# Five edits to an eight-stage network: first fill on ScalarE, causal mask on VectorE, six tiles of the ternary feed-forward begun early, expert weights by broadcast transfers

## The chip, the cores and the metric

The kernel runs on one core of one Trainium2 chip. The metric is the device time of one launch in microseconds (us), as the median of several runs. PE is the matmul engine (TensorE), DVE is VectorE, ACT is ScalarE, POOL is GpSimd, and SP is SyncE, which here mostly issues transfers. Each engine takes its own instructions in order and waits on semaphores for what other engines or transfers must have done.

## The reference, cut to what matters

The input `x` has 32 sequences of 64 rows and 256 columns, 2048 rows in all; `ctx` has the same shape. Four layers follow, each with an attention part and a feed-forward part, and each part adds its result to `x`:

```python
LN = _layernorm
x = x + L0_xattn(LN(x), ctx, ctx, gamma)  # A: 8 heads of 8 over the 64 rows, softmax over 256 columns
x = x + L0_ffn(LN(x))                     # B: gated feed-forward, 704 wide
x = x + L1_xattn(LN(x), ctx)              # C: 16 heads of 16, fake-quantised, softmax over all 2048 rows
x = x + L1_ffn(LN(x))                     # D: a block: causal attention, then 4 experts, top 2
x = x + L2_xattn(LN(x), ctx)              # E: 8 heads of 8 over 256 columns, |i - j| <= 64
x = x + L2_ffn(LN(x))                     # F: ternary feed-forward
x = x + L3_xattn(LN(x), ctx, ctx)         # G: sigmoid attention
x = x + L3_ffn(LN(x))                     # H: 8 experts, top 2, and shared experts
```

The parts that the change touches are these, shortened:

```python
# D, attention of each sequence, 16 heads of 128, after rotary encoding
scores = einsum('bhqd,bhkd->bhqk', q, k) / sqrt(128)
probs  = softmax(where(causal, scores, most_negative))
out    = einsum('bhqk,bhkd->bhqd', probs, v)

# F
rmsnorm(x, g)  = g * x * rsqrt(mean(x * x) + 1e-8)
act_quant(x)   = round(x * 127 / max|x|) / (127 / max|x|)     # one scale for each row
linear(x, w, g) = act_quant(rmsnorm(x, g)) @ ternary(w).T
out = linear(silu(linear(x, w1, g1)) * linear(x, w2, g2), w3, g3)   # 256 -> 1024 -> 256

# H
topk_w, topk_i = top_k(softmax(x @ gate_w.T), 2)
combine = zeros(N, 8), with topk_w at topk_i
h  = silu(x @ w_gate[e]) * (x @ w_up[e])                      # 8 experts, 176 wide
y  = sum over e of combine[:, e] * (h @ w_down[e])
y += (silu(x @ sw_gate) * (x @ sw_up)) @ sw_down              # shared, 352 wide
```

## The kernel before, in words

**Tiles and order.** The 2048 rows are 16 tiles of 128 rows by 256 columns, kept in SBUF through all stages as `xs[0]` to `xs[15]`; NG = 4 groups of four tiles are used where a matmul takes 512 rows. The stages run one after the other in the order A to H; G is done inside F's loop. On an engine the instructions stand in the order of the program. In A, C, E, F and the experts of D this order is written out by hand, under `tc.manual_schedule()`.

**A and E: `attention_slots`.** Both use one loop of slots `t`. Tile `i` begins its preparation at t = 8i - 2 and its score maxima at t = 8i + 16, its attention units at t = 8i + 30, its products at t = 8i + 32, and its normalisation and residual (`finish`) from t = 8i + 40 on; the loop ends at t = 180. A hook `start(t)` lets a stage put other work in a slot. The q and k of a tile are split into three bfloat16 parts, written to DRAM (`stacked`, d3q and d3k) and read back as stacked rows (`stack_rows`) into one of four buffer pairs `stk` and `stq`. These have their upper 64 rows filled once, with ones and with zeros (`operand_buffers`). In A (`row` is None) the fill is a DVE memset, L158, of the pair that belongs to each of the tiles 0 to 3, when the tile is prepared. In E the fill is a transfer from a filled row. All transfers of `stacked` and `stack_rows` (L212 and L220) are on SP's queue. The scores' maxima are matmuls (L251) with a DVE reduction each (L255); the exponentials are on ACT (L287).

**D attention.** 64 units, each one head by one group of 512 rows (four tiles). In slot `u` the PE does the product of unit u-4, the transposes of u-3, the scores of u-2 (`scores`), an output product, and the projections of unit u with their rotary encoding, which take DVE (`rtq`, `rtk`), ACT (`rwq`, `rwk`) and POOL. In `scores` the mask is a matmul: `identb` times `causalb`, L1097, is accumulated into the same PSUM bank as the four products q k (L1100). DVE then reduces the maximum (L1102), subtracts it (L1104), ACT takes one exponential over 128x512 (L1105), DVE sums (L1107), inverts (L1108) and multiplies (L1109).

**F.** `run_F` loops over slots t = 0 to 23. The list `parts` gives the order of steps in a slot, each with its lag in tiles. The first six steps of a tile, here called its front, are `deviations` (mean and variance, L1468), `first_factors` (factors with POOL's power), `first_sizes` (two products with gains, L1499, maximum and scales), `first_rounding` (two ACT activations), `first_transposes` (four on PE) and `first_copy` (ACT, L1521, giving `xT`). Then come `hidden_products` (L1529, eight matmuls) and `hidden` (L1544). The weights and gains of F are reserved and loaded in the stages ahead, in a pool `wp`.

**H.** For each group, 14 chunks of 128 columns of the experts' widths: chunks 0 to 10 are the routed experts (8 x 176 = 1408 columns), 11 to 13 the shared ones. A chunk is four matmuls for gate and up (L1844), for a routed chunk one matmul `cb` (L1848), and eight for the down product of the chunk before (L1820, `hout`). The routing weights of a group stand in `share`, in three bfloat16 parts; `cb` multiplies them with `owner`, a matrix of zeros and ones that says which column belongs to which expert, and so spreads them over the chunk's 128 partitions. DVE makes `hm` from up and silu(gate) (L1854), then multiplies it by `cb` (L1856). `owner` is filled by three ACT copies in F's last slots (L1760).

Of the kernel before, what the change touches and what calls it, by code (L numbers as in the profile page):

```python
# [9 lines left out]
F32 = mybir.dt.float32  # L10
# [7 lines left out]
P = 128  # L18
T = 2048
D = 256  # L20
# [11 lines left out]
def tile_net(ctx: ExitStack, tc: tile.TileContext, a: dict, out: bass.AP):  # L32
# [119 lines left out]
    def operand_buffers(pool, k, b, row=None):  # L152

        pair = {}
        for kind, value in (("k", 1.0), ("q", 0.0)):
            pair[kind] = pool.tile([P, 16, D], BF, name=f"st{kind}{b}")
            if row is None:
                V.memset(pair[kind][64:P], value)  # L158
            else:

                nc.sync.dma_start(pair[kind][64:P], bc(row[kind][64:P], 1, [64, 16, D]))
# [32 lines left out]

    def stacked(pool, k, dram, src, kind, i):
# [15 lines left out]
        for t in range(n):  # L211
            nc.sync.dma_start(d3[t].rearrange("d h c -> h d c"), t3[:, t % 3, :])  # L212
        return d3

    def stack_rows(k, d3, kind, i):
        st = k["st"][i % 4][kind]
        for m in range(3):
            first = 0 if kind == "q" else m
            src = d3[first : first + 3].rearrange("t d h c -> (t d) (h c)")
            nc.sync.dma_start(st[24 * m : 24 * m + 24], src)  # L220
# [807 lines left out]
    def run_D_attention(w, side, hs):  # L1028
# [4 lines left out]
        with ExitStack() as es:  # L1033
# [5 lines left out]
            causal = tpool.tile([P, 4, P], BF, name="causalb")  # L1039
            V.tensor_copy(causal, bc(w["causal"], 1, [P, 4, P]))  # L1040
# [53 lines left out]
            def scores(u):  # L1094
                qr, kr = qks.pop(u)
                sp = psum.tile([P, 4, P], F32, tag="sp", name="sp")
                PE.matmul(sp, identb, causal, start=True, stop=False, skip_group_check=True)  # L1097
                for j in range(4):
                    js = slice(j * P, (j + 1) * P)
                    PE.matmul(sp[:, j, :], qr[:, js], kr[:, js], start=False, stop=True, skip_group_check=True)  # L1100
                mx = pool.tile([P, 4], F32, name="mx")
                V.tensor_reduce(mx, sp, AX.X, ALU.max)  # L1102
                s = pool.tile([P, 4, P], F32, name="s", bufs=3)
                V.tensor_tensor(s, sp, bc(mx, 2, [P, 4, P]), ALU.subtract)  # L1104
                S.activation(s, s, AF.Exp, scale=scale)  # L1105
                sm = pool.tile([P, 4], F32, name="sm")
                V.tensor_reduce(sm, s, AX.X, ALU.add)  # L1107
# [178 lines left out]
    def first_of_E(w, psum):  # L1286
# [5 lines left out]
        for kind, value in (("k", 1.0), ("q", 0.0)):  # L1292
            row[kind] = cp.tile([P, D], BF, name=f"row{kind}")
# [35 lines left out]
    def run_E(w, side):  # L1329
        bd = w["bd"]  # L1330
        with ExitStack() as es:
# [38 lines left out]
            attention_slots(pool, psum, k, band, SCALE8, prepare, values, finish, early=EARLY)  # L1370
# [55 lines left out]
    def load_F(wp):  # L1426
# [3 lines left out]
        w["g3"] = bcast_row(wp, a["L2_ffn_g3"], 1024, "fg3")  # L1430
        return w

    def run_F(w, side):
# [10 lines left out]
        at = shared["atanh"]  # L1444
        t1, t2, t3 = (t.rearrange("p (c n) -> p c n", c=c) for t, c in zip(shared["tern"], (2, 2, 8)))
        with tc.tile_pool(name="Ft", bufs=1, side=side) as tpool, tc.tile_pool(
            name="Fw", bufs=2, side=side
        ) as pool, tc.tile_pool(name="Fp", bufs=1, space=PSUM) as psum, tc.manual_schedule():
            up = tpool.tile([P, 1], F32, name="rndup")
            V.memset(up, RND)  # L1450
            down = tpool.tile([P, 1], F32, name="rnddown")
            V.memset(down, -RND)
            st = [{} for _ in range(NT)]
            head = iter(())

            U = 1e-4 / 127.0
            base = [[tpool.tile([P, n + 1], F32, name=f"base{nm}{b}") for b in range(2)] for nm, n in (("a", 2), ("b", 1))]
            for tiles, lo in zip(base, (0, 2)):  # L1460
                for t in tiles:
# [506 lines left out]
```

## Time and profile before

| what | value |
|---|---|
| median of three runs | 2762.11 us (2757.15 to 2770.57) |
| the profiled execution | 2769.85 us, of which the instructions span 2768.1 us |
| mean granted TensorE clock | 0.977 of full speed |
| busy: PE | 2414.7 us (87%), its weight loads 1431.1 us |
| busy: DVE, ACT, POOL | 1856.7 us (67%), 1532.9 us (55%), 1534.5 us (55%) |
| A begins its first score product | 24.64 us |
| D attention | about 1205 to 1820 us, 9.31 us for one slot |
| E ends (last write of `x`) | 2276.0 us |
| H begins | 2453.5 us |

All times within the profile are counted from the start of its span. A row of the timeline reads: start, duration, engine, line and operation, what it writes and what it reads, the shape, how many were merged, and in brackets how long the engine sat idle before it and what ended the wait. A row of windows gives for one stretch the busy time of each engine with the number of instructions, then the granted clock, the share of DMA and GB/s. The lines are shown with the prediction, each where it is used.

### The profile page before, as it was taken

Reading aid. Unit: us, or ns where it says so; the run is one execution under the profiler, and the core shown is the slowest. Engines: PE = TensorE matmul, PEld = TensorE weight load, DVE = VectorE, ACT = ScalarE, POOL = GpSimd, SP = SyncE. Lnnn points to the kernel's source line nnn. Section 1 sums busy time; section 2 is a strip of 40 time slices with the busy share of each in tenths; the row PEclk is TensorE's granted clock in tenths of the full one; section 3 lists DMA queues with packets and bytes.
Section 4 is the critical chain, followed back from the end, with each engine's and each line's share of the span. In section 5 each row is a group of like instructions: output and inputs, shape, how many; then the busy total and the mean of one; then the engine's idle time right before and its main releaser. Section 6 shows DMA issues by size and latency. Waiting matters only on the chain.

```text
span 2768.1 us, 44270 instructions
## 1 busy us (share of the span) xinstructions
PE 2414.7 (87%) x15971; PEld 1431.1 (52%) x16078; DVE 1856.7 (67%) x3913; ACT 1532.9 (55%) x2181; POOL 1534.5 (55%) x1764
## 2 busy tenths in 40 slices
PE   4999889777777777779999999999888877789999
PEld 2555344344444444436666666666555544455565
DVE  7878555799999999955454554655577758833232
ACT  1666321699999999836555555534254557731111
POOL 4565533588888888865555555513488866710000
PEclk9999999999999999989999999999999998989999
DMA  6543000599999999930000000051343311000000
GB/s 166 133 116 86 24 1 1 120 204 204 202 204 200 203 206 201 204 106 1 16 8 23 8 1 1 1 107 52 79 99 90 93 46 55 1 0 8 8 8 8
DMA packets 618919, 227.89 MB, mean 82 GB/s; under 512 B 547494, under 2 KB 608844, under 8 KB 614092
## 3 DMA queue, kind: packets, MB, share of 16 engines
q1 hardware_dynamic: 615628, 224.26, 37.1%
q8 instruction: 127, 2.08, 0.3%
q10 hardware_dynamic: 3072, 0.79, 0.2%
q14 instruction: 92, 0.75, 0.1%
HBM read 66.91 MB, written 18.87 MB: 31 GB/s over the span
## 4 chain that ended last, share of the span: by engine, by line
PE 47%; DVE 19%; issue 9%; POOL 6%; ACT 2%; DMA 1%; ACTq 0%; POOLq 0%; DVEq 0%
DVE e L844 11%; PE yp L1141 4%; PE ppq L1082 4%; PE ppk L1082 4%; PE pgate L1844 4%; PE pup L1844 4%; PE hout L1820 3%; PE vp L1070 3%; POOL e L295 2%; PE sp L1100 2%; PE op L1126 2%; PE hmp L1198 2%; PE ep L1211 2%; PE sc L816 1%; PE op L805 1%
## 5 line engine op out<-in xcount | busy, mean ns | idle before, releaser
L868 ACT ACTIVATE ei<-e,nb,sq 128x2048 int16<-128x2048 f32 x256 | 535.4, 2092 | 39.6 <-DVE nb L865 35.0
L878 POOL CAST eb<-ei 128x2048 bf16<-128x2048 int16 x256 | 482.0, 1893 | 110.7 <-ACT ei L868 92.7
L816 PE MATMUL sc<-kT,qz 128*128 128x512 bf16 x930 | 281.0, 381 | 154.6 <-DVE e L844 150.6
L255 DVE TENSOR_REDUCE negm<-s 128x2 f32<-128x512 f32 (+1 forms) x512 | 300.7, 610 | 129.1 <-PE s L251 126.3
L844 DVE TENSOR_SCALAR_CACHE_REDUCE e<-sc,mx 128x1024 f32<-128x1024 f32 x256 | 326.1, 1274 | 0.4 <-DVE nb L865 0.3
L287 ACT ACTIVATE e<-s 128x1024 f32<-128x1024 f32 (+1 forms) x256 | 233.4, 916 | 152.4 <-PE s L283 103.5
L844 DVE TENSOR_SCALAR_CACHE_REDUCE e<-sc 128x1024 f32<-128x1024 f32 x256 | 312.4, 1220 | 4.8 <-PE sc L816 4.8
L816 PEld LDWEIGHTS <-qz 128*128 128x128 bf16 x1024 | 94.6, 97 | 260.0 <-issue 202.3
L251 PE MATMUL s<-stk,stq 96*128 96x256 bf16 (+1 forms) x1024 | 192.2, 271 | 41.0 <-DMA d3k<-t3k 24.6
L1090 POOL TENSOR_TENSOR rwq<-rwq,sin 128x512 f32<-128x512 f32 x64 | 81.1, 1267 | 239.2 <-ACT rwq L1087 212.3
L283 PE MATMUL s<-stq,stk 128*128 128x256 bf16 (+1 forms) x1024 | 180.8, 262 | 11.0 <-DMA d3k<-t3k 8.4
L829 PEld LDWEIGHTS <-vz 128*64 128x64 bf16 x4096 | 122.7, 109 | 113.7 <-issue 112.7
L1854 DVE TENSOR_TENSOR hm<-pup,sl 128x512 f32<-128x512 f32 (+1 forms) x56 | 38.7, 691 | 200.2 <-PE pup L1844 197.5
L1087 ACT ACTIVATE rwq<-ppq,dbq 64x512 f32<-64x512 f32 x128 | 87.4, 683 | 153.6 <-DVE rtq L1084 150.0
L1102 DVE TENSOR_REDUCE mx<-sp 128x4 f32<-128x512 f32 x64 | 44.3, 692 | 190.8 <-PE sp L1100 190.8
L829 PE MATMUL av<-eT,vz 128*64 128x128 bf16 x4096 | 163.2, 222 | 9.3 <-DMA eT<-eb 6.8
L251 PEld LDWEIGHTS <-stq 96*128 96x128 bf16 x1024 | 94.0, 101 | 131.6 <-issue 108.7
L305 PE MATMUL o<-e,vmo 128*32 128x256 f32 (+1 forms) x2048 | 150.7, 366 | 6.2 <-POOL e L295 4.8
L295 POOL TENSOR_SCALAR_AFFINE_SELECT e<-e 128x256 f32<-128x256 f32 (+1 forms) x256 | 132.9, 546 | 30.5 <-ACT e L287 30.3
L1852 ACT ACTIVATE sl<-pgate 128x512 f32<-128x512 f32 (+1 forms) x56 | 33.4, 597 | 207.9 <-PE pgate L1844 207.8
L91 POOL TENSOR_TENSOR rstd<-ve,mhalf 128x1 f32<-128x1 f32 (+1 forms) x40 | 25.9, 646 | 185.3 <-DVE ve L89 83.7
L1070 PE MATMUL vp<-Dwv,hnT 128*128 128x512 f32 x256 | 122.2, 600 | 6.1 <-ACT hnT L949 5.5
(406 smaller groups left out, 5443.1 us busy)
## 6 DMA issues: line engine op xcount, KB each, us to landing
stk<-d3k SPq DMA_DIRECT2D x96, 192.0 KB
stq<-d3q SPq DMA_DIRECT2D x96, 192.0 KB
d3k<-t3k SPq DMA_DIRECT2D x160, 64.0 KB
d3q<-t3q SPq DMA_DIRECT2D x96, 64.0 KB
eT<-eb SPq DMA_TRANSPOSE x256
fw<-in_L_ffn_w SPq DMA_DIRECT2D x3, 1024.0 KB
x<-in_x SPq DMA_DIRECT2D x16, 128.0 KB
c<-in_ctx SPq DMA_DIRECT2D x16, 128.0 KB
```

The lines of the kernel that those rows point to most:

```text
L251: PE.matmul(sc[:, hh, lo:hi], qs[0:96, 2 * hp + hh, qc * P : (qc + 1) * P], ks[0:96, 2 * hp + hh, lo:hi], start=band is None, stop=True, s ...
L255: V.tensor_reduce(negm[:, qc, 2 * hp : 2 * hp + 2], sc[:, :, lo:hi], AX.X, ALU.max, negate=True)
L287: S.activation(e[:, :, lo:hi], sc[:, :, lo:hi], AF.Exp, scale=scale)
L295: G.affine_select(e[:, :, s0:s1], e[:, :, s0:s1], [[0, 4], [step, s1 - s0]], ALU.is_ge, 0.0, base=base, channel_multiplier=chan,)
L816: PE.matmul(sc[:, k0 : k0 + 512], qz[i % 2][:, h, :], kT[:, h // 2, 1024 * part + k0 : 1024 * part + k0 + 512], start=True, stop=True,)
L829: PE.matmul(av[i][r0 : r0 + 64, h // 4, :], vz[:, kt, h // 4, h % 4, :], eT[:, kt, :], start=h == 0 and kt < 2, stop=h == H - 1 and kt >= ...
L844: V.tensor_scalar(e, scs.pop((n, part)), 1.0, mx[:, 0:1] if part else LOWEST, ALU.mult, ALU.max, accum_out=mx[:, part : part + 1],)
L868: S.activation(ei, es_.pop(n), AF.Exp, bias=nb, scale=sq[i][:, h : h + 1], accum_out=sums[i][:, h : h + 1],)
L878: G.tensor_copy(eb, eis.pop(n - 1))
L1070: PE.matmul(vp, hnT[g][:, c, j * P : (j + 1) * P], wv[:, c, :], start=c == 0, stop=c == 1)
L1082: PE.matmul(pp, wt[:, c, hh * P : (hh + 1) * P], hnT[g][:, c, :], start=c == 0, stop=c == 1)
L1844: PE.matmul(pp[:m], w[nm + "s"][:, c, cols], xnT[:, c, :], start=c == 0, stop=c == 1)
```

## The change

1. A's fill: `operand_buffers` fills the upper rows with `S.mul` of a row of ones by 1 or 0, on ACT, in place of the DVE memset.
2. A's transfers: for tile 0 the six transfers of q are issued from ACT's queue in place of SP's.
3. D's mask: the mask matmul and its bfloat16 tile go. DVE adds the mask while it brings the scores from PSUM to SBUF, reduces the maximum from there and scales it by -scale; ACT takes four exponentials of 128x128, each with its row's bias, and accumulates the sums on the way.
4. F's front: `front_of_F` holds the six steps, and `early_F` runs them for the tiles 0 to 5 from slot t = 147 of E on, two of the six steps of one tile in each slot, with `xT` and the scales `dqa` kept in `wp` and the transposes in PSUM under the tag "s1" of the score maxima. F's loop starts at t = 1 and leaves out the fronts of these tiles.
5. H's weights: `owner`, `share` in three parts and `cb` go. The routing weights of a group, 8 x 512 float32, are written to DRAM, and for every routed chunk SP issues one or two broadcast transfers into `wc` (128 x 512 float32, four buffers), three chunks ahead. The shared chunks stand first in each group.

```diff
@@ operand_buffers
             if row is None:
-                V.memset(pair[kind][64:P], value)
+                dst = pair[kind][64:P].rearrange("p h (a c) -> p (h a) c", c=P)
+                S.mul(dst, bc(ones[64:P], 1, [64, 32, P]), value)
...
+    def queue_of(k, kind, i):
+        return nc.scalar if kind == "q" and i == 0 and "row" not in k else nc.sync
...
-            nc.sync.dma_start(d3[t].rearrange("d h c -> h d c"), t3[:, t % 3, :])
+            queue_of(k, kind, i).dma_start(d3[t].rearrange("d h c -> h d c"), t3[:, t % 3, :])
...
-            nc.sync.dma_start(st[24 * m : 24 * m + 24], src)
+            queue_of(k, kind, i).dma_start(st[24 * m : 24 * m + 24], src)
@@ scores, D attention
-                PE.matmul(sp, identb, causal, start=True, stop=False, skip_group_check=True)
                 for j in range(4):
                     js = slice(j * P, (j + 1) * P)
-                    PE.matmul(sp[:, j, :], qr[:, js], kr[:, js], start=False, stop=True, skip_group_check=True)
+                    PE.matmul(sp[:, j, :], qr[:, js], kr[:, js], start=True, stop=True)
+                s = pool.tile([P, 4, P], F32, name="s", bufs=3)
+                V.tensor_tensor(s, sp, bc(w["causal"], 1, [P, 4, P]), ALU.add)
                 mx = pool.tile([P, 4], F32, name="mx")
-                V.tensor_reduce(mx, sp, AX.X, ALU.max)
-                s = pool.tile([P, 4, P], F32, name="s", bufs=3)
-                V.tensor_tensor(s, sp, bc(mx, 2, [P, 4, P]), ALU.subtract)
-                S.activation(s, s, AF.Exp, scale=scale)
+                V.tensor_reduce(mx, s, AX.X, ALU.max)
+                V.tensor_scalar(mx, mx, -scale, None, ALU.mult)
                 sm = pool.tile([P, 4], F32, name="sm")
-                V.tensor_reduce(sm, s, AX.X, ALU.add)
+                for j in range(4):
+                    S.activation(
+                        s[:, j, :], s[:, j, :], AF.Exp, bias=mx[:, j : j + 1], scale=scale, accum_out=sm[:, j : j + 1]
+                    )
@@ E's end
-            attention_slots(pool, psum, k, band, SCALE8, prepare, values, finish, early=EARLY)
+            front = []
+            def start(t):
+                if t == 147 and "F" in heads and "ternary" not in shared:
+                    front.append(heads.pop("F")(lambda name: psum.tile([P, 2, 2, P], F32, tag="s1", name=name, bufs=2)))
+                if front:
+                    next(front[0], None)
+            attention_slots(pool, psum, k, band, SCALE8, prepare, values, finish, start, early=EARLY)
...
+    FRONT = 6
+    def early_F(w, bank):
+        def own(shape, dt, name, i, bufs=2):
+            keep = name in ("xT", "dqa")
+            return w["wp"].tile(shape, dt, name=f"{name}_{i}" if keep else f"early_{name}", bufs=1 if keep else bufs)
+        fronts = front_of_F(w, own, bank)
+        w["done"] = FRONT
+        for s in range(FRONT + 2):
+            for k in range(3):
+                if 0 <= s - k < FRONT:
+                    for part in fronts[2 * k : 2 * k + 2]:
+                        part(s - k)
+                    yield
@@ run_F
-            for t in range(NT + 8):
+            for t in range(1 if done else 0, NT + 8):
                 for part, lag in parts:
+                    if part in fronts and t - lag < done:
+                        continue
...
-                    if with_g and t >= NT + 1 and part.__name__ == "gained":
-                        next(heads.get("owner", head), None)
@@ H
+        sh = pool.tile([8, 512], F32, name="sh")
+        S.copy(sh, tp[0:8].rearrange("e j t -> e (j t)"))
+        w["shares"][g] = w["dram"].tile([8, 512], F32, name="shd")
+        nc.sync.dma_start(w["shares"][g], sh)
...
+            ORDER = [11, 12, 13] + list(range(11))
+            def weights_of(n):
+                g, ch = divmod(n, 14)
+                ch = ORDER[ch]
+                if ch < 11:
+                    wc = wcs[n] = pool.tile([P, 512], F32, name="wc", bufs=4)
+                    e, r0 = ch * P // 176, 0
+                    while r0 < P:
+                        r1 = min(P, 176 * (e + 1) - ch * P)
+                        nc.sync.dma_start(wc[r0:r1], w["shares"][g][e : e + 1, :].to_broadcast([r1 - r0, 512]))
+                        e, r0 = e + 1, r1
...
-                    if ch < 11:
-                        cb = psum.tile([P, 512], F32, tag="cb", name="cb")
-                        PE.matmul(cb, owner[:, cols], sh, start=True, stop=True)
+                if n + 3 < 14 * NG:
+                    weights_of(n + 3)
...
-                    if ch < 11:
-                        V.tensor_tensor(hm, hm, cb, ALU.mult)
+                if n in wcs:
+                    V.tensor_tensor(hm, hm, wcs.pop(n), ALU.mult)
```

## The prediction

> **What bounds the kernel now.** I read the strip of forty slices first, then windows of the four touched stretches, then the timeline inside one slot of each.
>
> ```profile
> span 2768.1 us, 44270 instructions
> PE   4999889777777777779999999999888877789999
> DVE  7878555799999999955454554655577758833232
> ACT  1666321699999999836555555534254557731111
> 1280.00:1800.00 520.00, 518.61 (x2302) 346.78 (x2302) 275.42 (x466) 282.70 (x456) 283.04 (x226) 1.00 0.03 8
> 2249.50:2276.50 27.00, 18.46 (x178) 9.11 (x170) 9.82 (x20) 12.70 (x19) 16.60 (x31) 0.96 0.01 2
> 2276.50:2320.10 43.60, 27.30 (x103) 13.31 (x107) 34.15 (x104) 25.16 (x43) 21.37 (x32) 0.67 0.42 125
> 2453.50:2768.00 314.50, 310.78 (x1024) 182.89 (x1024) 88.33 (x180) 48.34 (x75) 8.81 (x11) 0.99 0.02 7
> ```
>
> A digit is the busy tenths of a 69 us slice. The window rows give stretch, length, busy us of PE, PE's weight loads, DVE, ACT, POOL, then clock and DMA. D's attention (1280 to 1800) and H (from 2453.5) are PE: 518.6 of 520 and 310.8 of 314.5, at full clock, with DVE and ACT about half used or less. There a PE instruction is worth its time. E's end has DVE at 9.8 of 27 us; F's start has DVE at 34.2 of 43.6, PE at 27.3 and a clock of 0.67: DVE is the limit, beside a pipeline that fills. Stage A's start is PE and ACT waiting:
>
> ```profile
> 24.64 1.01 PE L251 MATMUL s<-stk,stq 96*128 96x256 bf16 x4 [24.64 <-DMA d3k<-t3k]
> 26.87 3.47 DVE L158 MEMSET stk<- 64x4096 bf16 x1 [0.91 <-issue]
> 33.25 1.18 PE L251 MATMUL s<-stk,stq 96*128 96x256 bf16 x4 [6.66 <-DVE negm L255]
> 51.68 1.18 PE L251 MATMUL s<-stk,stq 96*128 96x256 bf16 x4 [6.61 <-DVE negm L255]
> 41.40 1.28 ACT L457 ACT_TABLE_LOAD   x1 [41.40 <-PE cT L101]
> 59.05 1.02 ACT L287 ACTIVATE e<-s 128x1024 f32<-128x1024 f32 x1 [14.17 <-DMA d3k<-t3k]
> ```
>
> Twice PE waits 6.6 us for a maximum (`negm`) queued on DVE behind two fills, and ACT does nothing until 41.4.
>
> **1, zeros on ACT, q's DMAs on ACT's queue (A): -6, from -11 to 0.** Eight DVE fills (3.47 and about 1.76) go; four of them, the two pairs at 26.87 and 45.29, lie behind PE's waits, so up to 2 x 5.6 = 11 comes free. ACT gains eight fills of 64x4096. The row for 128x2048 on ACT is 2.09 us, so twice that, 4.2 each, 33 us in all. The Trainium skill ("ScalarE: Activation LUTs", section "What ACT_TABLE_LOAD costs") gives an immediate-scale form 186 ns + 0.833 N ns, an estimate of 3.6 each or 29 us. Its section "Rules for kernel authors" speaks against the change: plain multiplies belong on VectorE. By that rule the move costs 29 for about 21 removed; by the trace those 29 to 33 fall into ACT's idle 41. I side with the trace, but not fully: the last fill ends near 33 to 40, and ACT's copies of cT and of the maxima, at 41.4 to 44 before, then come near 44. The row DMAs of tile 0's q wait on ACT behind two fills (8 us) and for t3q, and should issue at 18 to 20, against 16.61 on SP; the first product waited for k's transfers to 24.64, so it hardly moves (a late q costs 0 to 4). SP has six issues fewer ahead of tile 1's. The first exponentials at 59.05 move to about 50; tile 2's rows, still behind weight loads on SP (46.82), give 2 or 3 back. Hence -6.
>
> **2, causal mask on DVE (D): -13, from -14.5 to -8.**
>
> ```profile
> 1401.54 0.38 PE L1097 MATMUL sp<-causalb,identb 128*128 128x512 bf16 x1
> 1401.75 1.05 PE L1100 MATMUL sp<-rtk,rtq 128*128 128x128 f32 x8
> 1404.29 0.63 ACT L1105 ACTIVATE s<-s 128x512 f32<-128x512 f32 x1 [1.61 <-DVE s L1104]
> 1407.36 1.38 ACT L1087 ACTIVATE rwq<-ppq,dbq 64x512 f32<-64x512 f32 x2 [2.44 <-DVE rtq L1084]
> ```
>
> One slot of 9.31 us does one unit (a head, four tiles); 64 slots. The mask product lasts 0.38, but the next product starts 0.21 after it: 64 x 0.21 = 13.4, less 0.4 for slots at the ends. In its place DVE's add from PSUM takes the subtraction's 0.69, the sum's 0.69 goes, a 128x4 multiply of about 0.2 comes. ACT's one exponential becomes four of 128x128 with bias and accumulator. No such row exists: from below 0.29 each; from above the 128x128 row of L949 (0.454) plus the accumulator read of gjunk (0.20), 0.65 each. I take 0.42 (gjunk, 128x256 with an accumulator, starts its read 0.32 after itself, and has twice the columns): 1.7 against 0.63. The chain to the softmax is then +0.5 (at worst +1.4), and the transposes that read it come about 3.8 later. The ring that could bind is through ACT: exponentials 1.7, DVE's reciprocal and multiply 0.9, rtq 0.75, rwq and rwk 2.9, copies v, oT, pT about 1.7 = 8.0 against a PE slot of 9.10. At 0.65 each it is 8.9: still under. Where DVE runs beside POOL the multiply was once 1.72, not 0.69; such slots eat the rest, hence -8.
>
> **3, F's front of six tiles in E's last slots: -10, from -16 to 0.**
>
> ```profile
> 2269.43 1.76 DVE L322 RECIPROCAL rd<-rd 128x128 f32<-128x128 f32 x2 [5.29 <-ACT rd L318]
> 2275.99 0.48 DVE L1367 SCALAR_TENSOR_TENSOR x<-o,b_ct,x 128x256 f32<-128x256 f32 x1 [3.38 <-PE o L1365]
> 2276.46 0.43 DVE L1468 BATCH_NORM_STATS2 b<-x 128x6 f32<-128x256 f32 x1
> 2282.63 3.19 PE L1529 MATMUL l<-tern,xT 128*128 128x512 bf16 x7 [1.18 <-ACT xT L1521]
> 2320.05 1.40 DVE L1544 SCALAR_TENSOR_TENSOR h<-l,dqa,sl 128x512 f32<-128x512 f32 x2
> ```
>
> Removed from F: from E's last write to `h` of tile 4 at 2320.05 it is 43.6 us. The first product comes 6.1 after E's end; then each slot's DVE work is 7.9, of which 3.05 is a front (2276.46 to 2279.51). Without fronts the first product follows at once and a slot is near 4.8: about 24 us, -19.6. Added to E: six fronts of 2.95 and 0.7 of set-up are 18.4 us of DVE in slots with 17 us idle, and they stand in program order ahead of the last tile's reciprocal. From 2249.4 DVE then has 25.3 us to do before that reciprocal, so it starts near 2274.7, not 2269.43: +5.3. POOL's factors, ACT's rounding and PE's 24 transposes join as cross waits: I put +8. By the skill ("SBUF — State Buffer", section "Who interferes with whom") a DVE operation with two SBUF inputs and POOL lock each other out: E's own L327 ranges from 483 to 849 ns, so there are traces of it. Priced at +0.5 for each of the 12 gain products it is +6 more, so +11 in E. Row: -11.6; rule: -8.6. I take -10. If a front waits on PSUM (it shares tag s1, which the scores use), E stretches by a slot of about 10 and the gain is 0.
>
> **4, the ends of F: -0.5.** Three `owner` copies of 1.36 leave ACT; about 0.4 of one shows on the path to H.
>
> **5, H: -9.5, from -10 to -4.**
>
> ```profile
> 2510.90 1.88 PE L1844 MATMUL pgate<-xnT,hwgate 128*128 128x512 f32 x4
> 2514.34 0.38 PE L1848 MATMUL cb<-share,owner 96*128 96x512 bf16 x1
> 2514.55 1.89 PE L1820 MATMUL hout<-hwdown,hm 128*128 128x256 f32 x8
> 2516.28 1.88 PE L1844 MATMUL pgate<-xnT,hwgate 128*128 128x512 f32 x4
> ```
>
> A routed chunk starts 5.38 after the one before; a chunk without `cb` takes 5.17. 44 x 0.215 = 9.5. In its place each group writes its weights to DRAM and 18 broadcasts bring 256 KB a chunk. None in H's trace shows such a transfer; the nearest, `fg` rows (768 KB in three, issued from 1923.24), were gone by 1930, so about 2 us for 256 KB, against 15.5 us of lead (three chunks ahead) and three shared chunks at the head of each group that need none. The 72 broadcasts and four writes take SP about 0.43 each, 33 us of 314, and SP has only output stores beside them. DVE's multiply now reads two SBUF tiles, which by the same section of the skill could lock out with POOL; POOL works 8.8 of H's 314 us, so I leave it at 0.69. If cover failed, one chunk's wait each group, 4 x 1.4, gives the -4.
>
> **Sum**: -6 - 13 - 10 - 0.5 - 9.5 = -39. The profiled execution took 2769.85 (span 2768.1), 7.7 above the median of the three, so it would become 2731, and the median 2762.1 - 39 = 2723.
>
> **Rivals.**
> - *Only the PE removals count.* D and H give 22.5; A's gain goes back to late q rows, E's stretch equals F's gain. 2762 - 22.5 = 2740. For it: DVE has no room in E's last slots for 18 us. Against: F's slots are DVE-bound, so work that leaves them must show.
> - *All is uncovered.* A -11, F -16, D -14, H -10, F's ends -1: 2710. For it: both A waits are wholly behind fills. Against: tile 2's rows are late anyway.
> - *Slower: D's ring over ACT becomes the bound.* The four exponentials decide. They reach par with PE's 9.10 at about 0.70 each; at 0.90 the ring is 9.9, +0.6 over 60 slots against the old 9.31, +36, in place of -13. With A, E, F and H at -26 it is 2772. Against it: the dearest row says 0.65. Half of it (ring at par with the old slot, E and F at nothing) is 2750.
> - *It doesn't do what it says.* The instruction lists show the mask and cb products gone from PE and six fronts ahead of E's last writes, so little is left for this.
>
> **How the numbers follow.** Forecast 0.60 at 2723, only PE 0.18 at 2740, all uncovered 0.10 at 2710, half ring or par 0.05 at 2750, slower 0.07 at 2772. The low end, 2704, is the uncovered case less a 6 us scatter of three runs; the high end, 2750, takes in the second and fourth case with the costs at their upper bounds. A measurement here can tell about 0.5%, 14 us, so faster means under 2748: the first three cases less a little, 0.83; same 0.08; slower 0.09.
>
> **What would show it.** Right: D's slot 9.10 with ACT idle ahead of the exponentials; H's chunks 5.17 throughout and no wait for wc; the 6.6 us waits of L251 gone and the first e near 50; E's last write near 2284 less the earlier gains, with products of F right behind it. Wrong: exponentials over 0.65 apart, DVE waiting on DMA in H, the first L251 later than 28, or more than 11 us between the old end of E and the new one.

## The result, and the profile after

The changed kernel takes 2731.82 us (median of 2728.87 to 2736.45) against 2763.26 for the kernel before (2757.15 to 2770.57) on the same chip: a ratio of 0.9887, with a 95% interval of 0.9858 to 0.9916, or 31 us less, with an interval of 23 to 39. The two profiled executions differ by 40: that of before lay 6.6 us above its median, that of after 2.1 below its own. So a sum made on these two profiles explains 40 us, and 9 of them are scatter of the two executions.

Here are the span, the strip of forty slices, and the four stretches that were windowed in the prediction, now in the profile of after. The columns are: stretch, length, busy us of PE, weight loads, DVE, ACT, POOL, then clock, DMA share and GB/s.

```profile
span 2727.9 us, 44657 instructions
PE   4999889777777777779999999999898886889999
DVE  4878554799999999965555555646567777943332
ACT  5666321699999999947666666644254455831111
1270.00:1780.00 510.00, 508.38 (x2261) 338.22 (x2260) 266.77 (x465) 339.51 (x847) 283.26 (x225) 1.00 0.03 9
2241.80:2268.80 27.00, 19.27 (x138) 11.13 (x131) 19.51 (x52) 16.40 (x29) 13.64 (x27) 0.82 0.00 1
2268.80:2299.10 30.30, 19.26 (x80) 9.26 (x82) 18.78 (x46) 15.44 (x25) 15.40 (x20) 0.79 0.61 179
2422.80:2727.90 305.10, 301.23 (x980) 178.64 (x980) 94.36 (x209) 48.32 (x75) 3.76 (x4) 0.99 0.15 45
```

D's attention and H are still PE's (508.4 of 510, 301.2 of 305.1), only with less in them. In E's last 27 us DVE is now busy 19.5, where it was 9.8, and the clock there fell from 0.96 to 0.82. F's first stretch, to the `h` of tile 4, has shrunk from 43.6 to about 30 us.

From mark to mark, in us (a mark is the start of the first or last instruction of a row in each trace):

| stretch | before | after | difference |
|---|---|---|---|
| span's start to C's first score product | 506.8 | 499.8 | -7.0 |
| C, to D's first score product | 718.5 | 717.7 | -0.8 |
| D's first to last score product | 577.8 | 569.3 | -8.5 |
| D's experts and E's head, to E's first write of x | 233.8 | 231.1 | -2.7 |
| E's first to last write of x | 239.1 | 250.9 | +11.8 |
| E's last write to H's first product | 177.5 | 154.0 | -23.5 |
| H, to the span's end | 314.6 | 305.1 | -9.5 |

They add up to -40.2, the difference of the spans. Two rows carry little: the fourth ran from 227.9 to 236.6 in the twelve kernels below, none of which changes that stretch, so its -2.7 lies inside the scatter; and the first scatters by 11 us, as will be seen.

**D.** The rows of one slot's softmax in the timeline of after, with two of its four exponentials and the POOL product that runs beside it:

```profile
1302.82 1.06 PE L1103 MATMUL sp<-rtk,rtq 128*128 128x128 f32 x8
1303.91 0.69 DVE L1105 TENSOR_TENSOR s<-sp,causal 128x512 f32<-128x512 f32 x1 [2.73 <-PE sp L1103]
1304.67 1.27 POOL L1094 TENSOR_TENSOR rwk<-rwk,sin 128x512 f32<-128x512 f32 x1
1305.36 0.61 DVE L1108 TENSOR_SCALAR mx<-mx 128x4 f32<-128x4 f32 x1
1306.00 0.40 ACT L1111 ACTIVATE s<-s,mx 128x128 f32<-128x128 f32 x1 [0.92 <-DVE mx L1108]
1306.40 0.39 ACT L1111 ACTIVATE s<-s,mx 128x128 f32<-128x128 f32 x1
1311.92 1.06 PE L1103 MATMUL sp<-rtk,rtq 128*128 128x128 f32 x8
```

The score products of consecutive units stand 1311.92 - 1302.82 = 9.10 apart, not 9.31: the steady slot is what was forecast. The four exponentials start 0.39 apart (0.42 was taken), and ACT still waits for DVE ahead of the first, so the ring over ACT does not bind. The small multiply L1108 takes 0.61, though, where 0.2 was taken.

**A.** From the timeline of after: the last fill and what stood behind it on ACT, SP's queue, the first exponentials, and the product that waited, with its weight load:

```profile
35.24 0.78 PE L265 MATMUL nmT<-ident,negm 128*16 128x128 f32 x2
36.84 0.54 SPq L482 DMA_DIRECT2D wdown<-in_L_ffn_down_w  x1
37.18 3.60 ACT L160 ACTIVATE stq<-ones 64x4096 bf16<-64x4096 f32 x1
40.80 0.36 ACT L269 COPY nmr<-nmT 16x256 f32<-16x256 f32 x1
43.35 0.32 SPq L106 DMA_DIRECT2D sdown<-in_L_ffn_down_s  x1
43.77 1.83 SPq L218 DMA_DIRECT2D d3q<-t3q  x3
47.55 1.19 SPq L226 DMA_DIRECT2D stq<-d3q  x3
47.97 1.02 ACT L293 ACTIVATE e<-s 128x1024 f32<-128x1024 f32 x1 [6.54 <-PE s L289]
55.40 0.13 PEld L257 LDWEIGHTS <-stq 96*128 96x128 bf16 x2 [4.96 <-DMA stq<-d3q]
55.40 0.61 PE L257 MATMUL s<-stk,stq 96*128 96x256 bf16 x2 [4.48 <-DMA d3k<-t3k]
```

The 6.6 us waits are gone, and the first exponentials come at 47.97 instead of 59.05. The fills have a price on ACT as well: the maxima of the first tile are transposed by 36.02, but their copy (L269) runs at 40.80, right behind the last fill. How much earlier the first exponentials would come without those 4.8 us was not tried.

The next tile's first exponentials come 19.7 us after the first (at 67.6), against 13.6 before (59.1 to 72.6): of 11 us, 5 are left after one tile. Tile 2's q (`d3q`) was issued at 43.77, behind the last of B's weights at 43.35, and its rows (`stq`) at 47.55; the weight load for the product at 55.40 waited for these rows.

**E to F.** The last write of x, F's first products and the first and fifth `h`:

```profile
2268.77 0.48 DVE L1373 SCALAR_TENSOR_TENSOR x<-o,b_ct,x 128x256 f32<-128x256 f32 x1 [3.36 <-PE o L1371]
2269.30 0.59 PE L1581 MATMUL l<-tern,xT 128*128 128x512 bf16 x1 [0.57 <-DVE x L1373]
2272.09 1.28 ACT L1590 ACT_TABLE_LOAD   x1 [5.42 <-PE l L1581]
2274.11 1.41 DVE L1596 SCALAR_TENSOR_TENSOR h<-l,dqa,sl 128x512 f32<-128x512 f32 x2 [4.86 <-ACT sl L1590]
2279.88 1.40 DVE L1596 SCALAR_TENSOR_TENSOR h<-l,dqa,sl 128x512 f32<-128x512 f32 x2
```

F's products follow E's end by half a microsecond, where it was 6.6. The first `h` still takes 5.3, of which 1.28 is a table load; then a slot is 5.8.

**H.** Two routed chunks in the timeline of after:

```profile
2482.45 0.69 DVE L1904 TENSOR_TENSOR hm<-hm,wc 128x512 f32<-128x512 f32 x1
2488.78 1.88 PE L1893 MATMUL pgate<-xnT,hwgate 128*128 128x512 f32 x4
2493.94 1.88 PE L1893 MATMUL pgate<-xnT,hwgate 128*128 128x512 f32 x4
2499.10 1.45 PE L1893 MATMUL pgate<-xnT,hwgate 128*128 128x512 f32 x3
```

Chunks start 5.16 apart (2488.78, 2493.94, 2499.10), and the multiply by `wc` carries no wait.

### The profile page after: what moved, and what is told of

Its sections match the earlier page's. It is cut to its first block, busy times and chain, and to the rows that moved or that the text cites. A ratio compares the mean times of both kernels' runs of the same rounds, so it can differ in the third digit from the quotient of the medians.

```text
span 2727.9 us, 44657 instructions
## 1 busy us (share of the span) xinstructions
PE 2388.2 (88%) x15867; PEld 1414.6 (52%) x15970; DVE 1830.2 (67%) x3900; ACT 1620.8 (59%) x2634; POOL 1522.4 (56%) x1750
## 5 line engine op out<-in xcount | busy, mean ns | idle before, releaser
L822 PE MATMUL sc<-kT,qz 128*128 128x512 bf16 x930 | 281.0, 381 | 155.3 <-DVE e L850 151.4
L1105 DVE TENSOR_TENSOR s<-sp,causal 128x512 f32<-128x512 f32 x64 | 44.3, 692 | 165.4 <-PE sp L1103 165.4
L1111 ACT ACTIVATE s<-s,mx 128x128 f32<-128x128 f32 x256 | 99.6, 390 | 80.5 <-DVE mx L1108 80.5
```

The costliest lines, as they stand in the source:

```text
L822: PE.matmul(sc[:, k0 : k0 + 512], qz[i % 2][:, h, :], kT[:, h // 2, 1024 * part + k0 : 1024 * part + k0 + 512], start=True, stop=True,)
```

## The experiments

Each run is the changed kernel with one edit, unless said otherwise. Medians are compared with the kernel before on the same chip (2762.2 to 2766.1 in the runs below), and each stage by its marks. The column "first e of A" is the start of A's first exponentials; "C begins" takes in all of A and B.

| kernel | ratio to before (95%) | median | first e of A | C begins | D first to last | E first to last write | E's end to H | H |
|---|---|---|---|---|---|---|---|---|
| changed | 0.9887 (0.9858 to 0.9916) | 2731.8 | 48.0 | 499.8 | 569.3 | 250.9 | 154.0 | 305.1 |
| d_fold | 0.9863 (0.9843 to 0.9884) | 2727.4 | 49.4 | 500.7 | 565.5 | 250.4 | 155.2 | 304.6 |
| no_front | 0.9895 (0.9873 to 0.9918) | 2739.5 | 48.6 | 508.3 | 570.4 | 240.2 | 177.5 | 305.0 |
| fills_dve | 0.9878 (0.9859 to 0.9897) | 2734.0 | 59.4 | 501.4 | 569.6 | 251.9 | 154.3 | 305.2 |
| weights_later | 0.9859 (0.9841 to 0.9877) | 2727.8 | 49.2 | 501.2 | 570.7 | 250.7 | 153.3 | 305.0 |
| front_half | 0.9923 (0.9906 to 0.9940) | 2740.4 | 49.0 | 502.2 | 570.4 | 261.8 | 153.8 | 302.5 |
| weights_15 | 0.9883 (0.9868 to 0.9897) | 2729.4 | 50.8 | 499.2 | 568.9 | 250.7 | 155.3 | 304.6 |
| q_on_sp | 0.9893 (0.9877 to 0.9910) | 2731.9 | 48.9 | 497.2 | 570.0 | 251.5 | 156.8 | 305.1 |
| h_one_buf | 0.9893 (0.9872 to 0.9914) | 2732.1 | 49.1 | 502.2 | 569.0 | 250.9 | 156.6 | 305.2 |
| d_mask_only | 0.9868 (0.9854 to 0.9883) | 2728.5 | 48.3 | 497.6 | 567.7 | 252.4 | 156.1 | 302.5 |
| front_12 | 0.9896 (0.9875 to 0.9917) | 2739.1 | 49.2 | 499.3 | 569.8 | 258.8 | 156.4 | 304.6 |
| weights_132 | 0.9849 (0.9830 to 0.9867) | 2722.7 | 48.4 | 493.4 | 570.9 | 250.3 | 154.6 | 302.5 |
| both | 0.9845 (0.9832 to 0.9859) | 2722.7 | 48.5 | 496.6 | 565.5 | 250.7 | 154.0 | 305.1 |

Where nothing in a stage was edited, D agrees to 1 us either way (568.9 to 570.9), E to 1 (250.3 to 252.4), F to 2 (153.3 to 156.8). H took 302.5 in three kernels and 304.6 to 305.2 in the others, with no edit that could do it: in its first 10 us the granted clock was 1.00 in the three and 0.73 to 0.79 in the others. A scatters most: with A's code unchanged, C begins at 497.6 to 508.3. D, E and F can be read from one profile; A cannot, to better than some 5 us. The intervals of the ratios are 7 to 16 us wide, and all of them overlap with that of the changed kernel; so the whole times hardly tell these kernels apart, and the readings below rest on the marks.

What A's scatter goes with can be read in the traces. Past its first 60 us, A has none, one or two places where the granted clock falls to 0.50 for 3.4 us, at other places in each run. Here is the one of the changed kernel, and the stretch just ahead of it:

```profile
168.40:171.80 3.40, 1.75 (x18) 0.78 (x16) 2.65 (x6) 1.45 (x2) 0.37 (x1) 1.00 0.77 159
171.80:175.20 3.40, 3.17 (x18) 1.63 (x19) 1.57 (x6) 1.02 (x1) 0.55 (x2) 0.50 0.28 72
```

Each of these dips comes with a wait of PE for late rows, of 1.6 to 3.5 us, that began before it (here 1.9 us, to 172.0); other waits, of up to 2.5 us, had no dip. In the seven kernels with A's code unchanged, A's last exponentials start at 283.2 with no dip, at 285.1 to 287.1 with one, and at 287.9 to 291.3 with two. So runs of A are best compared at the same number of dips.

**D: the scale folded into the mask add (d_fold).**

```diff
-                V.tensor_tensor(s, sp, bc(w["causal"], 1, [P, 4, P]), ALU.add)
+                V.scalar_tensor_tensor(s, sp, scale, bc(w["causal"], 1, [P, 4, P]), ALU.mult, ALU.add)
-                V.tensor_reduce(mx, s, AX.X, ALU.max)
-                V.tensor_scalar(mx, mx, -scale, None, ALU.mult)
+                V.tensor_reduce(mx, s, AX.X, ALU.max, negate=True)
...
-                        s[:, j, :], s[:, j, :], AF.Exp, bias=mx[:, j : j + 1], scale=scale, accum_out=sm[:, j : j + 1]
+                        s[:, j, :], s[:, j, :], AF.Exp, bias=mx[:, j : j + 1], scale=1.0, accum_out=sm[:, j : j + 1]
```

> The changed kernel with D's scale folded into the mask add (scores x scale + mask in one DVE instruction, maximum taken with its sign turned), so the 128x4 multiply (628 ns on average where 0.2 us was estimated) is gone. Theory: D's slots are PE-bound at 9.10 us in the steady part and stay so; the first eight slots, 69.4 us between the first score rows against 67.2 before the change, are stretched by the longer chain and come down to about 67. First to last slot from 561.65 to about 559; the run 2 to 3 us shorter. Rival: it is ACT's four exponentials, not the multiply, that stretch the first slots: they stay at 69 and the run does not move.

The steady slot stayed at 9.10. The first eight slots, counted between DVE's first rows of each, came to 66.2 us (67.2 before, 69.4 in the changed kernel), and from the first such row to the last it was 557.8 against 561.7: 3.8 less. The theory stands for D; in the whole time the gain cannot be told from the scatter. What the multiply cost is in its row, of the changed kernel, by lowest, median and highest ns:

```profile
L1108 DVE TENSOR_SCALAR mx<-mx x64: 157/578/1280, 1226.8 to 1788.5; 128x4 f32<-128x4 f32 x64
```

Four numbers a partition take from 157 to 1280 ns. The trace shows what the rest is: in 52 of the 64 slots the multiply ends 24 to 33 ns after a POOL product that was running when it began (in the slot shown above, at 1305.97 after 1305.94); in the other twelve it took 157 to 172. So it is not work but waiting for POOL, counted inside the instruction.

**D: the mask on DVE, the softmax as it was (d_mask_only).**

```diff
                 V.tensor_reduce(mx, s, AX.X, ALU.max)
-                V.tensor_scalar(mx, mx, -scale, None, ALU.mult)
+                V.tensor_tensor(s, s, bc(mx, 2, [P, 4, P]), ALU.subtract)
+                S.activation(s, s, AF.Exp, scale=scale)
                 sm = pool.tile([P, 4], F32, name="sm")
-                for j in range(4):
-                    S.activation(
-                        s[:, j, :], s[:, j, :], AF.Exp, bias=mx[:, j : j + 1], scale=scale, accum_out=sm[:, j : j + 1]
-                    )
+                V.tensor_reduce(sm, s, AX.X, ALU.add)
```

> The changed kernel with D's mask added by DVE, but the rest of the softmax as it was: subtraction, one exponential of 128x512 and sum on DVE. Theory: the 0.21 us a slot come from the mask product that left PE and from nothing else; the slot is 9.10 us here too although DVE has 1.4 us more to do, and D from its first to its last score row stays within 2 us of the changed kernel's 561.7. Rival: only the four exponentials with their sums make room on DVE for the added mask; without them the softmax comes late for the transposes and the slot is longer than 9.31.

The slot was 9.10 here too, and first to last 560.0: the gain is the mask product that left PE, and the four exponentials add nothing to it. This run also shows what an operand's place costs. The same subtraction, first in the kernel before (one operand in PSUM), then here (both in SBUF):

```profile
L1104 DVE TENSOR_TENSOR s<-sp,mx x64: 690/691/693, 1233.9 to 1804.1; 128x512 f32<-128x512 f32 x64
L1108 DVE TENSOR_TENSOR s<-s,mx x64: 685/1186/1798, 1224.9 to 1784.9; 128x512 f32<-128x512 f32 x64
```

The best is the same, 0.69 us, the median 1.19. It is what the Trainium skill states in "SBUF — State Buffer", section "Who interferes with whom": a DVE instruction with two SBUF inputs locks with a POOL instruction that reads SBUF. The trace agrees: 58 of these 64 subtractions end 546 to 554 ns after a POOL product that was running when they began, and the other six took 685 to 693. D's slots have the room: the slot did not grow by it.

**F: no early fronts (no_front).**

```diff
-        heads["F"] = lambda bank: early_F(w, bank)
```

> The changed kernel without the early fronts (part 4 undone, the other four kept). Theory: the fronts cost E 11.8 us and save F 23.5 us, so E's part, from D's end to its last write, comes back by about 12 us and from there to H's first product it is 177 again: +11.7, about 2743. Rival: a good part of F's 23.5 came from elsewhere (the three owner copies that left ACT, the loop's first slot): F then stays near 165 us and the run gains nothing or gets shorter.

E's part went back to 240.2 (-10.7) and E's end to H back to 177.5, exactly that of before: the owner copies and the loop's first slot gave nothing. By its stages part 4 is worth 23.5 - 10.7 = 12.8 us, and by them the rival fell. The whole times do not show it clearly: by their ratios the two kernels lie 2 us apart, with overlapping intervals, while no_front is 5 to 12 us slower than the three kernels that were run beside it on its chip (d_fold, fills_dve and weights_later).

**F: the same fronts earlier and thinner (front_half).**

```diff
-                if t == 147 and "F" in heads and "ternary" not in shared:
+                if t == 111 and "F" in heads and "ternary" not in shared:
-                if front:
+                if front and t % 2:
                     next(front[0], None)
```

> The changed kernel with the same early fronts spread thinner and earlier: from slot t = 111 of E, one step in every second slot, so that they end where they now begin. Theory: E's stretch of 10.7 to 11.8 us is DVE work that finds no cover in E's last slots, while in the slots before PE is full (28.9 of 30 us) and DVE about 70% busy: there the 18 us lie beside PE's work, E's last part (first to last write, 250.9) comes down to about 243, F keeps its 154, and the run is some 8 us shorter. Rival: the cost is not DVE's lack of cover but the PSUM buffer shared with the score maxima, or the lock between DVE and POOL (72% busy there): then E stays at 251 or grows to 255 and more.

My theory fell: E grew to 261.8, 10.9 more than in the changed kernel and 21.6 more than without fronts. So slots with PE busy 92% and DVE 70% of the time (2158 to 2225 us of the changed kernel) had no cover for 18 us of DVE. PE's largest waits over the end of E, in us in total, times and longest, of this run:

```profile
PE s L253 <- DVE negm L261: 8.3, 11, 2.2
PE o L1364 <- DVE rd L335: 7.2, 5, 2.5
```

In the changed kernel the first is 2.3 over the same stretch, 2130 to 2270 us. The score products wait for DVE's maxima, whose two PSUM buffers the fronts' transposes now share. Which part of the 10.9 is the shared buffer and which is DVE being late was not separated. By slot 147 the maxima have ended (in the changed kernel the last one starts at 2226.8, the first row of the fronts at 2231.4), and DVE is also much idler from there on (9.8 of the last 27 us busy before); which of the two makes that place cheap stays open.

**F: twelve fronts (front_12).**

```diff
-    FRONT = 6
+    FRONT = 12
```

> The changed kernel with twelve early fronts instead of six. Theory: a front costs E's end 1.8 us (10.7 for six) and spares F about 2.7 us, the difference between a slot with a front (8.3) and without (5.6): E's part grows to about 262, F falls from 154 to about 138, and the run is some 5 us shorter. Rival: past the sixth tile F's slots are set by G's steps, which begin five slots in, and not by the front: F stays above 148, E grows all the same, and the run is 5 us longer.

The rival's numbers came (F at 156.4, E longer), but not its reason. E grew by 7.9 to 258.8, and then F's first product came only 11.7 us after E's last write: E's slots had run out, and the last fronts were done between the stages with PE waiting for them. From its waits, 2260 us on:

```profile
PE xqT L1525 <- ACT early_xq L1518: 7.9, 5, 2.2
```

Six more fronts cost 7.9 + 11.2 = 19 us there, and gave back 8.8 after F's first product, so fronts past the sixth tile still spare F something. Six is nearer than twelve to what E's last slots hold; numbers between were not tried.

**A: the fills on DVE again (fills_dve).**

```diff
-                dst = pair[kind][64:P].rearrange("p h (a c) -> p (h a) c", c=P)
-                S.mul(dst, bc(ones[64:P], 1, [64, 32, P]), value)
+                V.memset(pair[kind][64:P], value)
```

> The changed kernel with A's fills back as DVE memsets; tile 0's q transfers stay on ACT's queue. Theory: the two waits of 6.6 us of the score products for a maximum behind the fills return, the first exponentials come at 57 to 59 again instead of 48, and C begins 5 to 7 us later: about 2738. Rival: the gain of A comes from q's transfers on ACT's queue and the shorter queue of SP; then C begins within 1 us of the changed kernel's 499.8.

The waits returned as they were, 6.66 and 6.61:

```profile
33.59 1.18 PE L256 MATMUL s<-stk,stq 96*128 96x256 bf16 x4 [6.66 <-DVE negm L260]
52.02 1.18 PE L256 MATMUL s<-stk,stq 96*128 96x256 bf16 x4 [6.61 <-DVE negm L260]
59.38 1.02 ACT L292 ACTIVATE e<-s 128x1024 f32<-128x1024 f32 x1 [14.16 <-DMA d3k<-t3k]
```

but C began only 1.6 us later than in the changed kernel, and by its ratio the whole run is no slower (0.9878 against 0.9887). Both cases had expected something else: the fills are what moves the first exponentials by 11 us, and most of that is gone by A's end. Tile by tile, the first exponentials stand 11.4, 5.1, 5.8, 4.5, 5.5 us later than in the changed kernel for tiles 0 to 4, and 3.8 for the last: half is lost at tile 1. This run had no dip of the clock in A and the changed kernel one; against d_mask_only, which had none either, A's last exponentials come 5.7 us later (288.9 and 283.2). That the fills move the whole time is not shown.

**A: tile 0's q on SP's queue (q_on_sp).**

```diff
-        return nc.scalar if kind == "q" and i == 0 and "row" not in k else nc.sync
+        return nc.sync
```

> The changed kernel with tile 0's q transfers back on SP's queue; fills stay on ACT. Theory: the two waits of 6.6 us are gone because of the fills alone, and q's transfers on ACT's queue only keep the first product from coming later: it comes 1 to 2 us later here or at the same time, and A ends within 1.5 us of the changed kernel. Rival: the shorter queue of SP is half of A's gain: A's first exponentials come 3 us later or more, at 51 or after.

The first exponentials came 0.9 us later, the median was 2731.9: the same. Part 2 of the change is worth nothing that can be measured here.

**A: B's weights at another place (weights_later, weights_15, weights_132).** In the changed kernel the loads are issued at the preparation of tile 3; in these runs at tile 6, at tile 15, and at slot t = 132, after all rows.

```diff
-                if i == 3:
+                if i == 6:
                     pending.pop()()
```

> The changed kernel with the loads of B's weights issued at tile 6 of A instead of tile 3. Theory: of the 11 us that A wins at its first exponentials only 7 are left at its end, since tile 2's rows stand on SP's queue behind B's weights; with these later, the product waits of 4.5 us (55.4) and 3.2 us (46.5) go, and A ends about 4 us earlier: about 2728. Rival: tile 2's rows are late by their own way through DRAM, or another tile's rows are delayed instead: A's end moves by less than 1 us.

> The changed kernel with B's weights issued at A's last tile instead of tile 3, when the rows of all other tiles are under way. Theory: these 2 MB delay the rows of whatever tile is being prepared beside them by about 4 us (tile 2 in the changed kernel, tiles 3 and 4 in the run with the loads at tile 6); with the last tile they delay nothing that is needed soon, so the 11 us won at A's first exponentials are kept but for 2 or 3: A's last exponential at about 279 to 281 instead of 285.1. Rival: A's later tiles are held by the rows of the maxima on their own account, and the gain melts by tile 4 all the same: last exponential at 284 to 286. A second rival: B now waits for its weights; its start would show it.

> The changed kernel with the loads of B's weights issued after the last row transfers of A (slot t = 132). The run with the loads at the last tile kept 6 us up to its twelfth tile and lost them in the last ones. Theory: the loads cost whatever rows stand behind them on SP's queue, and here none does: the last exponential of A at 278 to 280 (285.1 in the changed kernel), the run 5 us shorter. Rival: A's later tiles are slowed by something else, such as dips of the granted clock: the last exponential again at 283 to 286.

With the loads at tile 6 the second tile came 14.2 us after the first (49.2 to 63.4), not 19.7; but the tiles from 78.7 on took 16.8 and 15.7 us, against 15.9 and 14.8 in weights_132, and the lag behind that run grew from 0.8 us at the first tile to 4.5 at the sixth: the rival, other tiles are delayed. With the loads at tile 15 A was 6 us ahead at its tenth tile (183.7 against 190.1) and lost it in 18.8 us for one tile near the end, with this wait of PE (B did not start later for its weights: from A's last exponentials to C it took 214.3 us, 214.7 in the changed kernel):

```profile
PE s L257 <- DMA d3q<-t3q: 3.5, 1, 3.5
```

Issued after all rows, the loads no longer delay any. Tile 2's q is issued at 34.72 in place of 43.77, from SP's queue of weights_132:

```profile
34.72 2.48 SPq L218 DMA_DIRECT2D d3q<-t3q  x3
```

The second tile's first exponentials come 14.0 us after the first, where every kernel with its fills on ACT and the loads at tile 3 has 19.1 to 20.5. So the place of the weights on SP's queue takes back half of what the fills win at A's start. At A's end, weights_132 stands at 278.6 with one dip, where the unchanged A has 285.1 to 287.1; the run `both` below, with the same place, at 281.4 with two dips, where it has 287.9 to 291.3. That is 6.5 us or more. C began at 493.4, the earliest of all runs, and the median, 2722.7, is the lowest of these kernels; its ratio of 0.9849 (0.9830 to 0.9867) still overlaps with that of the changed kernel, and weights_later has 0.9859.

**H: one buffer for the weights (h_one_buf).**

```diff
-                    wc = wcs[n] = pool.tile([P, 512], F32, name="wc", bufs=4)
+                    wc = wcs[n] = pool.tile([P, 512], F32, name="wc", bufs=1)
```

> The changed kernel with one buffer for H's broadcast weights instead of four, so that a chunk's transfer can start only when the chunk before has been multiplied. Theory: 256 KB take about 2 us and the issue up to 1, against 5.17 us from one multiply to the next: still hidden, H stays at 305 us. Rival: issue, transfer and completion together take more than 4.5 us, every routed chunk waits: H longer by 44 times the excess, 22 us for each half us. The idle time of DVE ahead of the multiply measures it.

H took 305.2. Its timeline around one issue:

```profile
2503.71 0.69 DVE L1904 TENSOR_TENSOR hm<-hm,wc 128x512 f32<-128x512 f32 x1
2504.43 0.34 SPq L1863 DMA_DIRECT2D wc<-shd  x1
2524.35 0.69 DVE L1904 TENSOR_TENSOR hm<-hm,wc 128x512 f32<-128x512 f32 x1
2525.07 0.79 SPq L1863 DMA_DIRECT2D wc<-shd  x2
2529.51 0.69 DVE L1904 TENSOR_TENSOR hm<-hm,wc 128x512 f32<-128x512 f32 x1
```

The issue follows the multiply that frees the buffer (2524.35 + 0.69, then 2525.07), and the next multiply runs at 2529.51, right behind its own `hm`: issue and landing fit into 4.4 us. H as a whole did not grow, so the cover is there with one buffer; four are more than enough.

**Both gains together (both):** d_fold and weights_132.

> The changed kernel with the two edits that shortened it, D's folded scale and B's weights issued after A's last rows. If they add up, D's part is 3.8 us and A's 6.5 us shorter than in the changed kernel, and the run is at about 2720, 0.984 to 0.985 of the kernel before. If later stages take it back, as A's middle took back the gain of its start, it stays at 2727 or more.

2722.71, a ratio of 0.9845 (0.9832 to 0.9859), below the changed kernel's 0.9887 (0.9858 to 0.9916), with intervals that just touch. D keeps its 3.8, at 565.5. A was at 496.6 this time, inside its scatter. The run does not tell the sum from the later loads alone (2722.68).

## Why the prediction was right, point by point

The forecast was -39 and a median of 2723; the profiles give -40, the medians -31. That -39 and -40 agree is in part luck: 9 of the 40 are scatter of the two executions, and 3.5 lie in stretches that no edit touches (C, and D's experts). By their stages A is worth 1 to 6 us, D 8.5, E and F 11.7 and H 9.5, in all 31 to 36, which fits the medians. The mechanism of each part held, but for the small ones that gave nothing (tile 0's q, the ends of F); the mis-sized terms are D's multiply, what A gives back, and both halves of E and F.

- **A, -6 (0 to -11).** The mechanism held: both waits went, the first exponentials came 11 us earlier, and tile 2's rows behind B's weights gave some back. The give-back was the mis-sized term: 6 us at once instead of "2 or 3", while the start won 11 instead of about 9. The -7.0 between the two profiles is no confirmation: with two dips of the clock each, A's last exponentials come 1 to 4 us later in the kernel before than in those with the changed A, and fills_dve gives 5.7 with none. A fill took 3.61 us, as the immediate-scale form of the Trainium skill's "ScalarE: Activation LUTs", section "What ACT_TABLE_LOAD costs", had it (3.6), not the 4.2 by the trace's row, whose scale and bias are tiles. Most fills fell into ACT's idle time, as taken, but the last held up the copy of the first tile's maxima by 4.8 us. The late q of tile 0 cost nothing.
- **D, -13 (-8 to -14.5).** The steady slot fell by 0.21 as worked out, and the ring over ACT stayed far off: 0.39 an exponential. D came out at -8.5 between score products. The term that failed is "a 128x4 multiply of about 0.2": it took 0.63 on average, waiting for POOL, in a chain that the first eight slots wait for. d_fold, without it, gives -12.3, by the score products and by the DVE rows alike. The low end, -8, had been left for DVE beside POOL, but for another multiply, the one over 128x512. The Trainium skill's "SBUF — State Buffer", section "Who interferes with whom", which I weighed for E, says that `tensor_scalar`, the kind of this multiply, can lock with POOL too, where its operands allow a two-port mode; the 52 waits for POOL agree with it, and I did not ask it here.
- **E and F, -10 (-16 to 0).** -11.7, from +11.8 and -23.5 where +8 and -19.6 stood: both halves were too small by nearly 4 us, and that they cancel is luck. One of the prediction's own signs of being wrong came with it, more than 11 us at E's end. For E's stretch the rows had given +8 and the rule of "Who interferes with whom" +11. That +11 is itself a slip: 6 more on top of +8 is +14; 11 is 6 on top of the 5.3 from which the +8 had started. The price was off too: the gain products took 670 ns on average in E against 478 in F, so 12 x 0.19 = 2.3 us, not 6. The clock fell as well (0.96 to 0.82); what else makes up the 11.8 was not separated. Of F's gain, 14.5 lie before the `h` of tile 4 (from 44.1 to 29.6 us after E's end, not 24): the five slots took 5.3, 5.8, 5.8, 4.9 and 7.7 where 4.8 each had stood, and over half of the excess is the fifth, where G's steps begin. Another 2.1 came in F's middle and 6.9 at the other end, from the last `h` to H (42.4 to 35.5), which no step had. They belong to the early fronts: no_front, with all other parts of the change, has 42.4 again. In the 10 us ahead of H's first product the granted clock was 0.50 before (2443.5 to 2453.5) and 0.75 after (2412.8 to 2422.8). By what way the fronts shorten F's tail was not tried.
- **F's ends, -0.5.** Nothing: no_front has no owner copies and the old 177.5.
- **H, -9.5.** -9.5, with the granted clock at 0.74 in H's first 10 us in both profiles. The transfers are hidden, with one buffer too.
- **The rivals.** "Only the PE removals count" fell by the stages of no_front: the fronts are worth 12.8 us there. "All is uncovered" fell by what A gave back and by E's +11.8. The slower side (four exponentials at 0.90) was far off, at 0.39 apart.

## What to carry to other kernels

Where one engine fills a stage, an instruction taken from it is worth its start-to-start time, and such terms (D's slot, 9.10 as worked out, and H's chunk, 5.16 for 5.17) can be trusted; a gain won at a latency-bound start must be followed tile by tile, since the next late transfer takes it back. Weights for the next stage cost whatever stands behind them in their queue: issue them after the last transfer that is waited for soon. Average idle time of an engine is not yet room: six fronts fit better where the ring of maxima had ended, and the same work in slots with 30% of DVE idle cost 11 us more. A tiny DVE instruction beside a busy POOL can cost the rest of a POOL product; on the chain of a pipeline that fills, folding it into its neighbours gave back 3.8 us.

## What the runs showed of the hardware that I had not expected

- A DVE instruction on 128x4 numbers took 157 to 1280 ns beside a busy POOL, median 578, and in 52 of 64 cases ended 24 to 33 ns after the POOL product that it had begun under. A 128x512 subtraction took 0.69 us with one operand in PSUM and 1.19 in the median with both in SBUF.
- The start of F without early fronts ran at a granted clock of 0.75, 0.50, 0.50 and 0.54 over four windows of 10 us, with them at 0.67, 0.61, 0.83 and 1.00 (2260 to 2300 us of either run). How much of what early work gave is this clock was not separated.
- In A, waits of PE for late rows of 1.6 to 3.5 us were followed, in some places of each run and not in others, by 3.4 us at a granted clock of 0.50. Identical code then began C up to 11 us apart.
